# The order of the transposes, value projections and weight pieces in a slot-attention and FFN kernel, changed in one step

## Chip, cores and metric

The kernel runs on one core of a Trainium2 chip. The metric is the device time of one execution in microseconds; the time before is 1460.58 us, the median of three runs (1460.13 to 1461.77).

## What is computed

For four sequences of 512 tokens and 512 channels the program computes a pre-norm attention block over 64 slots (16 heads, key size 64, value size 128) and a pre-norm FFN with weights rounded to fp8, each with its residual. Cut to what matters:

```
q, k, v, s = x_ln @ Wq, x_ln @ Wk, x_ln @ Wv, clip(x_ln @ Ws, -32, 32)     # by heads
z = cumlogsumexp(s);  g = exp(z[t-1] - z[t]);  p = exp(s - z)
hk[t] = hk[t-1] * g[t] + k[t] p[t]^T;     ok[t] = (q[t] * 64**-0.5) @ hk[t]
hv[t] = hv[t-1] * g[t] + p[t] v[t]^T;     o[t]  = softmax(ok[t]) @ hv[t]
o = o * rsqrt(mean(o**2) + 1e-5) * g_norm * silu(x_ln @ Wg)
x = x + o @ Wo
x = x + ((silu(x_ln2 @ f8(gate) * gs) * (x_ln2 @ f8(up) * us)) @ f8(down)) * ds
```

## The kernel before

**Units.** The attention runs in 32 units (g, b): g is a pair of heads (0 to 7), b a sequence. All g run over the sequences 0 and 1 in turn, (0,0), (0,1), (1,0), (1,1) and so on, then all g over 2 and 3. A unit is one call of `attention` (the first is `first_unit`). v is projected for two pairs of heads at once, so that units of even g are **long** (they have four blocks of v, `X.values(0)` to `(3)`), and those of odd g are **short**. The output of a unit is finished in the next one: `before.scale_output`, `scale_other`, `turn_output`, `high_output`, `split_output`, `low_output`, `project_output` and `add_output` belong to the unit before. After the units comes the FFN.

**fp32 by parts.** A product of fp32 values is made from rounded parts: every weight matrix and every activation is held as a high part, a rest and a mixed part, and a projection (`Projection`) is eight 512-column matmuls (`main`, ps_s and so on) and four more (`mixed`, ps_s_m), in two PSUM tiles of the pool `proj`, which has three buffers. ACT reads the first (L525, for v L587), DVE subtracts the second (L547, for v L588).

**The head of a unit.** s is projected, clipped and exponentiated (eT), then k and q are projected. Beside them on DVE and ACT: the sums of squares of the last read-out (L796, L797), their power on POOL (L800), the scaling of the last output (`scale_output` L805 on DVE, `scale_other` L811 on ACT), and the scan z (L680) with its logarithm and reciprocal (L681, L682 on ACT). Then eT, kT and the two halves of the scaled output are transposed on PE (`turn_e` ps_e, `turn_k` ps_kn, `turn_output` ps_oT, four matmuls each), into three PSUM banks that are taken in turn (`bank`), and copied out: e (L692) and kn (L697) by ACT, the output by DVE (L834). `query_key` makes the four diagonal blocks a (ps_a; DVE L618), `key_states` the running sums sk (ps_sk; DVE L639 and L641, POOL L705).

**The tail.** Two gates (ps_g), the slot scores (ps_ok, okT L731), `value_states` (ps_sv), `softmax` (ps_okn, then DVE L738 and L740), the projected output of the unit before in four blocks (ps_o), `softmax_exp` (ACT), `slot_weights` (ps_w, wT L762), `weight_slot` (ps_b, DVE L618 again), `softmax_sum`, `read_out` (ps_ov).

**The list of pieces.** Work that isn't bound to a place stands in a list, `work`, and is issued in small pieces. `other(n)` issues the next n (or `pace[0]`), `piece()` issues until one that isn't a mere beginning, `need(name)` issues until none of that name is left. In the first half (b of 0 and 1) the pieces split the weights of the next units: `nm_` is the first high part on ACT (L256), `nm` one rest on DVE (L263 or L265, and L268), with the next high part and, where a buffer comes free, a fetch and the write of the parts by SP. They are put on the list by `load`: s, k, q and g in units with b = 1, v there too where g is even, o in units with b = 0. In the second half the parts are read back by DMA, and the pieces are the rounding of the FFN's weights ("round": `first`, `second`, `third`, two DVE instructions each, L463 to L477). Every engine takes its instructions in the order in which the program issues them, so that the place of `other` in the code is the place of the piece in its engine's queue.

**Layer norms.** The next sequence's normalised tokens (xn) are measured (m), normalised and transposed in four `steps`, taken by `next_step` or `early_step`; `step(n)` needs normalise(n), transposes (ps_xn L356) and puts the split of the parts (`xs_b`) and normalise(n+2) on the list. These steps run in (0,0), (7,0), (7,1), (0,2), (7,2), (7,3) and in the FFN. `turned()` says that an xs piece is next on the list. `pace[0]` is 2 in (0,1), (7,0), (0,2) and (7,2), else 1.

**Start.** The first sequence is fetched in four blocks by SP, with two halves of the first v matrix (`fetch`) behind block 0; block 0 is normalised, transposed and used for `values(0)` before block 1.

Of the kernel before, what the change touches and what calls it, by code (L numbers as in the profile page):

```python
# [49 lines left out]
def kernel(  # L50
# [268 lines left out]
    def layernorm(b, which, n_bank=None, first=None):  # L319
# [33 lines left out]
        def transposes(n):  # L353
            pt = bank(f"ps_xn{which}_{b}_{n}", n_bank).rearrange("p (c t) -> p c t", c=KC)
            for c in range(KC):
                nc.tensor.transpose(pt[:, c, :], xn[n][:, c * P : (c + 1) * P], ident)  # L356
            hi = dst[0][:, :, n * P : (n + 1) * P]
            if start:
                nc.scalar.copy(whole[0][:, :, n * P : (n + 1) * P], pt)
            elif which == 1:  # L360
                nc.scalar.mul(hi, pt, UNDER)
            else:
                nc.scalar.copy(hi, pt)
            pts[n] = pt
# [517 lines left out]
    def first_unit():  # L882
# [43 lines left out]
        next_step()  # L926
        next_step()
        X.softmax()
# [3 lines left out]
        X.slot_weights()  # L932
        other(1)
        X.gate_silu(0)
        X.gate_silu(1)
        exp_and_log()
        X.weight_slot()
        X.softmax_sum()
        need("xs_0")
        piece()  # L940
        piece()
# [3 lines left out]
    def attention(g, b, before, load, gated):  # L945
# [22 lines left out]
        def running_sum():  # L968
            before.scale_other()
            X.running_sum()  # L970
            if first:
                other(1)
            else:
                small()
# [5 lines left out]
        need("q")  # L980
        X.queries(other if even or turned() else None)
        load("q")
        X.turn_e()
        if even:
            X.turn_k()
            next_step()
            if turned():
                other(1)
            need("v")
            X.values(0)  # L990
            X.values(1)
            before.turn_output(0)
            before.high_output(0)
            before.turn_output(1)
            before.high_output(1)
            X.key_states()
            X.inverse()
            X.query_key()
            other()
            X.values(2)  # L1000
            before.split_output(0)
            next_step()
            other()
            X.values(3)
            other()
            next_step()
            before.split_output(1)
        else:
            before.turn_output(0)
            X.turn_k()  # L1010
            before.turn_output(1)
            before.high_output(0)
            before.high_output(1)
            X.query_key()
            X.key_states()
            before.split_output(0)
            before.split_output(1)
            X.inverse()
            if work and work[0][1] is scale_low:
                other(1)  # L1020
            if work and work[0][0] == "o":
                other()
# [21 lines left out]
        X.softmax()  # L1044
        if not turned():
            small()
        need("o")
        before.project_output(0)
# [13 lines left out]
        X.softmax_sum()  # L1062
        if even or b > 1 or steps:
            other()
        next_step()
        if turned():
            other(1)
        X.read_out()
        return X

# [80 lines left out]
    with tc.manual_schedule(engines=EVERY):  # L1151
        blocks = x[0].rearrange("(n p) d -> p n d", p=P)
        x1[0] = two.tile([P, NT, D], F32, tag="v", name="x1_0")
        for n in range(NT):
            nc.sync.dma_start(x1[0][:, n, :], blocks[:, n, :])
            if n == 0:
                fetch()
                fetch()
# [11 lines left out]
        for i, (g, b) in enumerate(units[1:], 1):  # L1170
# [44 lines left out]
            elif g % 2:  # L1215
                if not turned():
                    piece()
# [4 lines left out]
            else:  # L1222
                other(1)
                other(1)
            before = attention(g, b, before, load, gated)
# [90 lines left out]
```

## Time and profile before

The profiled execution took 1460.69 us; its span, from the first to the last instruction, is 1459.0 us, at a mean granted TensorE clock of 0.998.

| unit | start of ps_s, us | length to the next start, us |
|---|---|---|
| (0,1) long | 58.11 | 42.81 |
| (1,0) short | 100.92 | 30.95 |
| (1,1) short | 131.87 | 30.39 |
| (2,0) long | 162.26 | 41.13 |
| (2,1) long | 203.39 | 41.15 |
| (3,0) short | 244.54 | 30.97 |
| (3,1) short | 275.51 | 30.38 |
| (7,0) short, two steps | 531.74 | 32.76 |
| (7,1) short, two steps | 564.50 | 32.08 |
| (0,2) long, four steps | 596.58 | 43.54 |
| (0,3) long | 640.12 | 41.21 |
| (2,2) long | 742.09 | 41.57 |
| (2,3) long | 783.66 | 42.07 |
| (3,2) short | 825.73 | 30.38 |
| (7,2) short, two steps | 1114.75 | 32.17 |
| (7,3) short, two steps | 1146.92 | 31.37 to the first ps_fg at 1178.29 |

How to read the views: a line of the timeline has the start in us from the span's start, the time to the end of the last of the merged instructions, engine, source line, operation, what is written and read, shape, count, and in brackets how long the engine had been idle and what ended that. PE is the matmul engine, PEld its weight loads, DVE, ACT, POOL and SP the vector, scalar, GpSimd and sync engines. In the list of waits a line names who waited for whom, with the sum, the number and the longest of the waits in us.

### The profile page before, as it was taken

What the parts mean: (1) busy time and instruction counts of PE and PEld (TensorE: products, weight loads), DVE (VectorE), ACT (ScalarE), POOL (GpSimd) and SP (SyncE); (2) the same over time, 40 slices, a digit from 0 to 9 for tenths busy, and PEclk for the clock granted to TensorE, in tenths of its full rate; (3) what the DMA queues carried; (4) which work ended last, traced back from release to release, by engine and by line L of the source; (5) the groups of instructions that cost most, each with busy time, mean ns of one, the idle gap of its engine ahead of it and who ended that gap; (6) DMA issues with size and microseconds to landing.
All of it is one profiled execution on the core that took longest, in us unless ns stands there. A gap on an engine that the chain in (4) does not pass through costs nothing.

```text
span 1459.0 us, 22764 instructions
## 1 busy us (share of the span) xinstructions
PE 1431.5 (98%) x8875; PEld 1178.1 (81%) x8875; DVE 1105.6 (76%) x1966; ACT 711.0 (49%) x1214; POOL 242.4 (17%) x271
## 2 busy tenths in 40 slices
PE   8999999999999999999999999999999999999998
PEld 4688888888888888888888888888888888888886
DVE  6788768976897689878988898898889874445333
ACT  4556555555565556455544454456445643222221
POOL 2012211211121122211211121111112120000000
PEclk9999999999999999999999999999999999999999
DMA  8275456565656464456546654665465562101000
GB/s 332 78 226 176 143 159 172 174 191 157 173 173 191 128 231 123 138 159 188 159 116 188 202 166 102 195 202 168 129 180 174 148 178 28 59 0 58 1 29 29
DMA packets 80715, 212.51 MB, mean 146 GB/s; under 512 B 6152, under 2 KB 34848, under 8 KB 75424
## 3 DMA queue, kind: packets, MB, share of 16 engines
q1 hardware_dynamic: 62080, 177.49, 32.8%
q0 software_dynamic: 18528, 33.58, 15.7%
q8 instruction: 70, 1.15, 0.3%
q14 instruction: 37, 0.30, 0.1%
HBM read 107.23 MB, written 108.00 MB: 148 GB/s over the span
## 4 chain that ended last, share of the span: by engine, by line
PE 85%; DVE 10%; ACT 2%; issue 1%; DMA 1%; POOL 0%; SPq 0%; DVEq 0%; ACTq 0%
PE ps_o L861 8%; PE ps_g L520 8%; PE ps_v L579 7%; PE ps_fg L1077 6%; PE ps_fu L1077 6%; PE ps_o_m L861 4%; PE ps_ov L785 4%; PE ps_g_m L543 4%; PE ps_v_m L579 4%; PE ps_s L520 3%; PE ps_k L520 3%; PE ps_q L520 3%; PE ps_fd L1126 3%; PE ps_fe L1126 2%; PE ps_b L614 2%; PE ps_a L614 2%
## 5 line engine op out<-in xcount | busy, mean ns | idle before, releaser
L877 POOL DMA_DIRECT2D stream<-y x128 | 113.2, 893 | 471.5 <-DVE y L876 464.3
L861 PE MATMUL ps_o<-w_o,oT 128*128 128x512 f32 x512 | 144.8, 404 | 0.0
L520 PE MATMUL ps_g<-xs,w_g 128*128 128x512 f32 x496 | 125.2, 394 | 0.0
L579 PE MATMUL ps_v<-w_v,xs 128*128 128x512 f32 x480 | 122.4, 397 | 0.3 <-ACT v L587 0.3
L1098 DVE SCALAR_TENSOR_TENSOR h<-ps_fu,scol,act 128x512 f32<-128x512 f32 x48 | 36.0, 751 | 105.4 <-PE ps_fu L1077 104.1
L871 ACT ACTIVATE y<-ps_o 128x512 f32<-128x512 f32 x128 | 76.7, 599 | 73.9 <-PE ps_o L861 73.9
L520 PEld LDWEIGHTS ps_g<-xs,w_g 128*128 128x128 f32 x496 | 91.7, 188 | 19.8
L861 PEld LDWEIGHTS ps_o<-w_o,oT 128*128 128x128 f32 x512 | 91.5, 188 | 17.1
L579 PEld LDWEIGHTS ps_v<-w_v,xs 128*128 128x128 f32 x480 | 87.7, 188 | 19.5 <-ACT v L587 0.8
L705 POOL COPY sk_both<-sk 64x192 f32<-64x192 f32 x64 | 43.7, 682 | 344.6 <-DVE sk L641 342.7
L1077 PE MATMUL ps_fg<-xs,wf 128*128 128x512 f32 x384 | 96.5, 393 | 0.0
L1077 PE MATMUL ps_fu<-xs,wf 128*128 128x512 f32 x384 | 95.0, 389 | 0.0
L876 DVE TENSOR_TENSOR y<-y,ps_o_m 128x512 f32<-128x512 f32 x128 | 87.2, 682 | 10.1 <-ACT y L871 9.3
L587 ACT ACTIVATE v<-ps_v 128x512 f32<-128x512 f32 x60 | 35.9, 599 | 99.5 <-PE ps_v L579 99.5
L1077 PEld LDWEIGHTS ps_fu<-xs,wf 128*128 128x128 f32 x384 | 72.1, 188 | 15.2
L795 ACT ACTIVATE og<-ps_ov 128x512 f32<-128x512 f32 x64 | 38.1, 597 | 93.4 <-PE ps_ov L785 93.4
L1077 PEld LDWEIGHTS ps_fg<-xs,wf 128*128 128x128 f32 x384 | 71.1, 188 | 14.4
L588 DVE TENSOR_TENSOR v<-v,ps_v_m 128x512 f32<-128x512 f32 x60 | 41.1, 684 | 53.6 <-PE ps_v_m L579 53.6
L861 PE MATMUL ps_o_m<-w_o,oT 128*128 128x512 f32 x256 | 79.3, 391 | 0.2 <-ACT y L871 0.2
L1104 ACT CAST both<-h 128x512 fp32r<-128x512 f32 x48 | 29.8, 620 | 96.5 <-DVE h L1098 96.5
L800 POOL TENSOR_TENSOR rs<-rs,mhalf 128x8 f32<-128x8 f32 x32 | 59.2, 1850 | 86.5 <-DVE rs L797 48.4
L1095 ACT ACTIVATE act<-ps_fg,scol 128x512 f32<-128x512 f32 x48 | 33.0, 688 | 81.2 <-PE ps_fg L1077 81.2
(171 smaller groups left out, 3309.5 us busy)
## 6 DMA issues: line engine op xcount, KB each, us to landing
stream<-y POOLq DMA_DIRECT2D x128, 256.0 KB, 6.1
split_v<-w_v SPq DMA_DIRECT2D x4, 3072.0 KB, 14.7
split_g<-w_g SPq DMA_DIRECT2D x8, 1536.0 KB, 6.9
split_o<-w_o SPq DMA_DIRECT2D x8, 1536.0 KB, 6.2
w_v<-split_v SPq DMA_DIRECT2D x4, 3072.0 KB, 15.6
w_g<-split_g SPq DMA_DIRECT2D x8, 1536.0 KB, 6.5
w_o<-split_o SPq DMA_DIRECT2D x8, 1536.0 KB, 9.7
rounded<-qw SPq DMA_DIRECT2D x36, 256.0 KB, 3.9
```

The lines of the kernel that those rows point to most:

```text
L520: nc.tensor.matmul(self.p, products(self.nm, c, self.col0, i), xs[self.b][i][:, c, :], start=(i == 0 and c == 0), stop=(i == 1 and c == KC ...
L543: nc.tensor.matmul(self.m, products(self.nm, c, self.col0, 2), xs[self.b][2][:, c, :], start=(c == 0), stop=(c == KC - 1),)
L579: nc.tensor.matmul(dst, xs[b][i][:, c, n * P : (n + 1) * P], wt["v"][:, i, c * 2 * HV : (c + 1) * 2 * HV], start=(i == which[0] and c == 0 ...
L614: nc.tensor.matmul(pa[h][:, n, :], lT[rows, cols], rT[rows, cols], start=True, stop=True)
L785: nc.tensor.matmul(po[h][:, n, :], self.bb[h][:, n, :], both_v[self.b][:, n, self.v0 + h * DV : self.v0 + (h + 1) * DV], start=False, stop ...
L800: nc.gpsimd.tensor_tensor(rs, rs, mhalf.rearrange("p (h n) -> p h n", h=HG), ALU.pow)
L861: nc.tensor.matmul(dst, self.oT[:, i, h, n * P : (n + 1) * P], wt["o"][:, i, h * D : (h + 1) * D], start=(i == which[0] and h == 0), stop= ...
L871: nc.scalar.mul(y, p, 1.0 + DELTA)
L876: nc.vector.tensor_tensor(y, y, m, ALU.subtract)
L877: nc.gpsimd.dma_start(stream[self.b][n * P : (n + 1) * P, :], y, accum_op=ALU.add)
L1077: nc.tensor.matmul(pp, w[:, c * P : (c + 1) * P], xs[b][k][:, c, :], start=(c == 0 and k == 0), stop=(c == KC - 1 and k == 1),)
L1126: nc.tensor.matmul(sums[n], parts[k][:, n * P : (n + 1) * P], fw[c][2], start=(c == 0 and k == 0), stop=(c == NFC - 1 and k == 1),)
```

## The change

Six things are moved, none is added or left out of the computation.

1. Both kinds of unit now begin the same way after q: `turn_e`, `turn_output(0)`, `turn_k`, `turn_output(1)`, the two highs of the output, then (after the step of a layer norm, in long units) `query_key` and `key_states`. In long units the four blocks of v follow, with the output's splits and inverse between them; before, two blocks of v stood between the transposes of e and k and those of the output, and key states and a followed these.
2. Pieces in long units: the one between q's parts goes (unless an xs piece is due), one to three are issued after `values(0)` (three in (0,1), two for b of 2 and 3, one else), and for b of 2 and 3 one instead of two before the unit. In (0,1) none is left in `running_sum`.
3. Pieces elsewhere: short units with b = 0 lose the piece at their start; long units with b = 1, except the first, issue `piece()` for `other()` after softmax and after `softmax_sum`.
4. Steps of the layer norms: in short units of the first half the last step comes after `read_out`; in those of the second half it is dropped there, and an `early_step` is added after `key_states`.
5. `first_unit`: the fourth step goes from behind `value_states` to behind `slot_weights`, the xs piece that it makes is issued after `weight_slot`, and one `piece()` before the read-out goes.
6. Start: one half of v's matrix is fetched after block 0 and one after block 1, and the first copy of xn is made in two halves.

```diff
             if start:
-                nc.scalar.copy(whole[0][:, :, n * P : (n + 1) * P], pt)
+                for half in (0, 1) if n == 0 else (None,):
+                    cs = slice(None) if half is None else slice(half * KC // 2, (half + 1) * KC // 2)
+                    nc.scalar.copy(whole[0][:, cs, n * P : (n + 1) * P], pt[:, cs])
...
         X.value_states()
         next_step()
-        next_step()
         X.softmax()
         X.softmax_exp()
         other(1)
         X.gate_main(1)
         X.slot_weights()
-        other(1)
+        next_step()
         X.gate_silu(0)
         X.gate_silu(1)
         exp_and_log()
         X.weight_slot()
+        need("xs_1")
         X.softmax_sum()
         need("xs_0")
-        piece()
         piece()
         X.read_out()
...
             X.running_sum()
-            if first:
-                other(1)
-            else:
+            if not first:
                 small()
...
-        X.queries(other if even or turned() else None)
+        X.queries(other if turned() else None)
         load("q")
         X.turn_e()
+        before.turn_output(0)
+        X.turn_k()
+        before.turn_output(1)
+        before.high_output(0)
+        before.high_output(1)
         if even:
-            X.turn_k()
             next_step()
             if turned():
                 other(1)
+        X.query_key()
+        X.key_states()
+        if even:
             need("v")
             X.values(0)
+            other(3 if first else 2 if b > 1 else 1)
+            before.split_output(0)
             X.values(1)
-            before.turn_output(0)
-            before.high_output(0)
-            before.turn_output(1)
-            before.high_output(1)
-            X.key_states()
             X.inverse()
-            X.query_key()
             other()
             X.values(2)
-            before.split_output(0)
+            before.split_output(1)
             next_step()
             other()
             X.values(3)
             other()
             next_step()
-            before.split_output(1)
         else:
-            before.turn_output(0)
-            X.turn_k()
-            before.turn_output(1)
-            before.high_output(0)
-            before.high_output(1)
-            X.query_key()
-            X.key_states()
+            if b > 1:
+                early_step()
             before.split_output(0)
...
         X.softmax()
-        if not turned():
+        if even and b == 1 and not first and not turned():
+            piece()
+        elif not turned():
             small()
+        elif not even and b > 1:
+            other(1)
...
         X.softmax_sum()
-        if even or b > 1 or steps:
+        if even and b == 1 and not first and not turned():
+            piece()
+        elif even or b > 1 or steps:
             other()
-        next_step()
-        if turned():
-            other(1)
+        if even:
+            next_step()
+            if turned():
+                other(1)
         X.read_out()
+        if not even and b < 2:
+            next_step()
+            if turned():
+                other(1)
         return X
...
-            if n == 0:
-                fetch()
+            if n < 2:
                 fetch()
...
             elif g % 2:
-                if not turned():
+                if b > 0 and not turned():
                     piece()
...
             else:
-                other(1)
-                other(1)
+                other(1 if b > 1 else 2)
             before = attention(g, b, before, load, gated)
```

## The prediction

> **What bounds the kernel now.** I read the page's span and busy shares, then the list of PE's waits, then the timeline of PE for the start of every unit (its first ps_s row), and last the timeline of all engines inside units that run longer than their like.
>
> ```profile
> span 1459.0 us, 22764 instructions
> PE 1431.5 (98%) x8875; PEld 1178.1 (81%) x8875; DVE 1105.6 (76%) x1966; ACT 711.0 (49%) x1214; POOL 242.4 (17%) x271
> ```
> PE sets the end. In the timeline a group of eight 512-column matmuls starts 1.81 us before the next (ps_k 247.38, ps_k_m 249.19), 227 ns each, everywhere. The change adds and removes no PE work, so only PE's waits and the seams between its groups can move. The Trainium skill (Trainium Kernel Development and Optimization, Performance Expectations) calls matmul busy time a bad measure and weight-load busy time a good one; by its rule the 81% of PEld would leave 19% of the span, an estimated 277 us, to a better order, while the 227 ns pitch says that nothing of this is open here.
>
> ```profile
> PE ps_xn L356 <- DVE xn L349: 3.6, 4, 1.3
> PE ps_kn L596 <- DVE kT L547: 2.3, 4, 0.7
> PE ps_xn L356 <- DVE b L618: 2.0, 2, 1.2
> PE ps_oT L596 <- ACT e L692: 1.1, 3, 0.4
> ```
> Columns: total us, times, longest. The lengths of the units (start to start) show the rest: an undisturbed long unit takes 41.13 (162.26 to 203.39), a short one 30.38 (275.51 to 305.89). Over that are (0,1) by 1.7; (1,0), (3,0), (5,0) by 0.57 each; (2,2) 0.44, (2,3) 0.94, (4,2) 0.94, (4,3) 0.80, (6,2) 0.84, (6,3) 0.46; and the units with transposes of xn. The short units' 0.57 and the excess of the second half come from these rows, of the timeline of (3,0) and of (2,3):
>
> ```profile
> 244.54 2.09 PE L520 MATMUL ps_s<-xs,w_s 128*128 128x512 f32 x8
> 247.56 1.96 POOL L800 TENSOR_TENSOR rs<-rs,mhalf 128x8 f32<-128x8 f32 x1 [2.54 <-DVE rs L797]
> 250.50 1.23 DVE L680 TENSOR_TENSOR_SCAN z<-eT 128x512 f32<-128x512 f32 x1
> 252.54 0.63 ACT L682 ACTIVATE rzT<-rzT 128x512 f32<-128x512 f32 x1
> 253.08 0.61 ACT L256 ACTIVATE w_v<-raw_v 128x512 fp32r<-128x512 f32 x1
> 253.60 0.58 ACT L525 ACTIVATE qT<-ps_q 128x512 f32<-128x512 f32 x1
> 254.07 0.58 ACT L692 COPY e<-ps_e 128x512 f32<-128x512 f32 x1
> 254.71 0.66 PE L596 MATMUL ps_oT<-ident,og 128*128 128x128 f32 x4 [0.36 <-ACT e L692]
> ...
> 793.19 0.66 PE L596 MATMUL ps_kn<-ident,kT 128*128 128x128 f32 x4 [0.65 <-DVE kT L547]
> ```
> Four transposes in turn (e, oT0, kn, oT1) use three banks, so oT1 takes e's bank and starts 0.64 after the ACT copy of e does. That copy stands on ACT behind L682, any weight high (L256) and qT, and these hang on the DVE scan z. Undisturbed, oT1 starts 9.59 after the unit (e at +8.28, three groups of 0.44): **the copy of e must start by +8.95**. Here it starts at +9.53.
>
> **The change, part by part.** Times with + are from the unit's start; the price of a weight pair on DVE (L263, L268) is 1.33 (247.30, 248.02, next 248.63), of an ACT high 0.53.
>
> Long units, second half (b of 2 or 3). One DVE piece leaves the head (other(1) for two) and one leaves queries; both go behind values(0). Then the head is that of the short units (1,2) to (5,3), which have the same order and one piece there, and whose lengths are 30.31 to 30.39, without stall. All 0.44+0.94+0.94+0.80+0.84+0.46 = **-4.4** goes. What is late next is the DVE queue in the v blocks. From the start of the first v block (0): its L588 can run at 3.16 (793.60 to 796.69, and 0.07 for the seam), then two pieces (0.67, 1.06 or 1.33 each), split 1.33, L588 0.61, inverse 1.35, a piece, L588, split, a piece, the last L588. A third proj buffer must be free at 13.77. With the pieces third-first-second the last L588 starts at 13.36 and frees it at 13.96, else before: 0.2 in (0,3), (2,3), (4,3), **+0.6**. Below, nothing; above, with all four pieces at 1.33, 1.15 a unit. Behind a waiting L588 on DVE stand the split of the output and inverse; who waits for them is ACT's low_output and okT, both behind the gates, 5 us later. The moved pieces take their SP issues along (0.34 for a split write, 0.37 for a fetch); no wait of PE names these. On POOL sk_both comes 8 us earlier in long units, ahead of stream adds that are issued much later: 0.
>
> Seams. Old long order over bare matmuls: e 0.44, kn 0.35, v +0.10, oT pair 0.96, sk 0.50, a 1.09, v +0.14 = 3.58. The short order: 0.44+0.44+0.44+0.55+1.09+0.50+0.16 = 3.62. 15 long units at 0.04: **+0.6**.
>
> Long units of the first half with b=1: (2,1), (4,1), (6,1). Their head is unchanged, two o pairs, and in the old order nobody waited for e's copy, since kn was followed by v. Now oT1 does. The timeline of (2,1):
>
> ```profile
> 203.39 2.09 PE L520 MATMUL ps_s<-xs,w_s 128*128 128x512 f32 x8
> 211.64 0.63 ACT L682 ACTIVATE rzT<-rzT 128x512 f32<-128x512 f32 x1
> 212.18 0.61 ACT L256 ACTIVATE w_s<-raw_s 128x512 fp32r<-128x512 f32 x1
> 212.70 0.58 ACT L525 ACTIVATE qT<-ps_q 128x512 f32<-128x512 f32 x1
> 213.18 0.58 ACT L692 COPY e<-ps_e 128x512 f32<-128x512 f32 x1
> ```
> The copy starts at +9.79, so oT1 at 10.43 for 9.59: 0.84. Their softmax piece now puts two highs on ACT ahead of exp, 0.1 more. Three units: **+2.8**. (2,0), (4,0), (6,0) have the copy at 9.08, after a high that queries issued and no longer does; less 0.5 it is on time: 0.
>
> (3,0), (5,0): the piece at their start goes (b > 0), and the new tail piece of (2,1) leaves rs where it was (L797 at +2.68). Then POOL's pow binds L805: 5.18 becomes 5.05, 0.13 each; up to 0.3 with the 4.89 of (7,0). **-0.3**.
>
> (1,0): without the start piece, the first v pieces fall to running_sum: v_ is an ACT high behind L682, and the DVE pair waits for it ahead of kT. z at +5.78, L682 7.82, high 8.36 to 8.97, pair 9.0 to 10.33, kT to 11.0; kn at 11.0 for 9.16, oT1 at 11.45 for 10.17: **+1.3**. (1,1) then inherits v at its start, o_ with o at running_sum, and o behind inverse: high 7.54 to 8.15, pair, kT to 10.2, kn +1.05; the late o pair holds okT as in (7,1), where sv to okn is 1.62 for 0.96: **+1.7**.
>
> In all of these the low end is 0, if the piece comes sooner than I count, and the high end half as much again, if qT is late with it.
>
> (0,1): DVE work 1.33 shorter ahead of rs, no high before qT, but three pairs behind v block 0; the e stall falls from 0.23 and the v_m waits (0.50 and more) go; new waits by the same count as above 0.05+0.6+0.5, and 0.25 at oT1. 1.7 becomes 1.5: **-0.2**, between -0.9 and +1. (0,2): measure, parts and n2 come between the transposes and a on DVE, some 2.5 us; a's reader pok comes 14 us later: 0.
>
> (0,0): x block 1 is fetched ahead of half of raw_v. Its landing (DVE's stats wait for it to 9.68) stops binding, but measure(2) stands before normalise(1) on DVE, and block 2 lands as before, some 7.7 after its issue at 2.7 (the blocks take 7.5 in the median, 7.9 at most), at 10.4; 1.0 of measure and 0.6 of normalise later the transposes start at 12.04 for 12.29, **-0.25**; the halved copy of xn feeds a v product that isn't on this path: 0. One xn step moves from before okn to behind w. okn needs okT at 47.75, now 48.73: 1.0, of which 0.44 is the xn now in the hole from w to b (52.64 to 54.02): **-1.0**.
>
> The granted clock was 0.50 from 15.27 to 18.69, after a stretch with PE busy 1.82 of 3.41: 1.7 lost, which I leave where it is; gone or doubled it is -1.7 or +1.7. The Trainium skill (TensorE: Matmul & The Clock Gate, Part 1) says that the window runs free of the program; by it the sum could shift by that estimate either way without cause in the code.
>
> (7,0), (7,2): step 1 held the read-out behind b (1.53 and 0.95 in ps_b, 1.23 of it as idle before ps_xn). In (7,0) it goes behind read_out; 1.1 comes back, but DVE is full through (7,1) to its ps_a at +11.25, and gives only what rs gains, 0.5: **-0.5**. (7,2) **-1.1**. Step 3 of (7,3) now stands behind key_states and calls normalise(3) there: on DVE behind both a and three sk.
>
> ```profile
> 1159.26 1.29 DVE L618 TENSOR_TENSOR a<-ps_a,tri 128x512 f32<-128x512 f32 x2 [0.33 <-PE ps_a L614]
> 1159.66 2.14 PE L520 MATMUL ps_g<-xs,w_g 128*128 128x512 f32 x8
> 1160.71 0.48 DVE L641 TENSOR_TENSOR sk<-ps_sk,sk 128x64 f32<-128x64 f32 x2
> ```
> PE is free at 1159.66; DVE ends sk at 1161.1, normalise takes 0.54: PE stands 2.0. With 0.15 at oT1: **+2.15**.
>
> Sum: -4.4-0.3-0.2-0.25-1.0-0.5-1.1 = -7.75; +0.6+0.6+2.8+1.3+1.7+2.15 = +9.15; net +1.4. The profiled execution took 1460.69 (span 1459.0 and 1.69 around it), 0.11 over the median 1460.58: 1462.1, or **1462.0** beside the median. FFN: no edit reaches it, and its weights come as before.
>
> **The rivals.** *Faster (1456.2).* The late pieces I found in heads don't bind: the weight highs are ready before I place them, so (1,0), (1,1), (2,1), (4,1), (6,1) keep their lengths: 1462.0 less 2.8, 1.3 and 1.7 is 1456.2. For: the head of short units bears one pair. Against: the rows above have the high between L682 and qT, and (3,0) shows oT1 waiting at +9.53. *Slower (1467.3).* The v blocks: DVE's in-order queue holds L588 and so the proj buffers; from a last L588 later than 13.1 each unit pays. With 0.35 in each of 15 long units, 1462.0+5.3. For: all DVE idle time of the old v blocks (2.29, 2.04) is spent by then. Against: my count leaves 0.1 to 1.5 to spare in most. *No effect of the head:* the second-half stalls stay, because kT is late by the running_sum piece and not the head's: 1466.4. Against: short units with that piece have none.
>
> **How the numbers follow.** A measurement here tells 0.2% (2.9 us) from nothing. Within it (1457.7 to 1463.5): 0.48, its own range 1459.5 to 1463.5. Faster 0.22. Slower: v blocks 0.20, head 0.10. Two in ten left out, with the clock's 1.7: 1456.0 to 1466.0.
>
> **What would show it.** After: no wait of kn for kT in (2,2) to (6,3); oT1 waiting 0.8 for e in (2,1), (4,1), (6,1); kn waiting for kT over 1 us in (1,0) and (1,1); xn waiting 2 us for L349 in (7,3); (0,0) 1.2 shorter. Wrong if the v blocks show ps_v or ps_g waiting for DVE v L588 in many units, or if these waits are absent.

## The result, and the profile after

The changed kernel takes 1466.14 us (median of six runs, 1464.88 to 1466.58), the kernel before on the same chip 1460.16 (six runs, 1458.67 to 1461.77). The ratio is 1.0041, with a 95% interval of 1.0031 to 1.0051: **slower by 0.4%**. The profiled execution took 1466.44 us, its span is 1464.7. The page of the changed kernel, span and busy times:

```profile
span 1464.7 us, 22809 instructions
PE 1434.7 (98%) x8875; PEld 1178.8 (80%) x8875; DVE 1108.7 (76%) x1966; ACT 710.6 (49%) x1215; POOL 230.0 (16%) x271
```

The engines do the same work as before. (PE's 3.2 us more are no more matmuls: the count is equal. Each of the two profiles has one stretch of 3.41 us at half clock inside the program, so that this isn't the difference.) The list of PE's waits, changed kernel; lines of the code from 361 on stand two further down than before, so that L596 is now L598 and L547 is L549:

```profile
PE ps_xn L356 <- DVE xn L349: 3.5, 3, 2.1
PE ps_oT L598 <- ACT e L694: 2.4, 4, 0.7
PE ps_kn L598 <- DVE kT L549: 2.1, 2, 1.2
...
PE ps_g_m L545 <- ACT sg L527: 1.4, 1, 1.4
...
PE ps_g_m L545 <- ACT v L589: 0.9, 1, 0.9
```

Three things are read from it. kn waits for kT 2 times now, not 4, and the sum is hardly less; but these are other places: the four of before stood in the second half and are gone, the two of now stand in (1,0) and (1,1). oT waits for e 2.4 us in place of 1.1, in (0,1), (2,1), (4,1) and (6,1). And two waits stand here that the list of before doesn't have: the gates' ps_g_m for ACT, once 1.4 and once 0.9 us. The unit lengths (start of ps_s to the next), with the forecast's term beside what came:

| place | before | after | forecast | measured |
|---|---|---|---|---|
| from the span's start to the first ps_s | 20.39 | 17.87 | -0.25 | -2.51 |
| (0,0) | 37.73 | 36.81 | -1.0 | -0.91 |
| (0,1) | 42.81 | 45.99 | -0.2 | **+3.18** |
| (1,0), (1,1) | 30.95, 30.39 | 31.72, 32.11 | +1.3, +1.7 | +0.77, +1.73 |
| (2,1), (4,1), (6,1) | 41.15 each | 42.20 each | +0.98 each | +1.05 each |
| (2,0), (4,0), (6,0) | 41.13 each | 41.21 each | +0.04 each | +0.08 each |
| (3,0), (5,0) | 30.96 each | 30.37 each | -0.15 each | -0.60 each |
| (7,0), (7,1) | 32.76, 32.08 | 31.73, 33.10 | -0.5 in sum | -0.01 in sum |
| (0,2), (0,3) | 43.54, 41.21 | 43.73, 41.41 | +0.3 in sum | +0.39 in sum |
| (2,2), (2,3), (4,2), (4,3), (6,2), (6,3) | 251.20 in sum | 248.44 | -3.75 | -2.76 |
| (7,2) | 32.17 | 30.73 | -1.1 | -1.45 |
| (7,3) | 31.37 | 36.24 | +2.15 | **+4.87** |
| FFN | 280.70 | 280.71 | 0 | +0.01 |

The two bold rows lie 6.1 us over their terms. That is more than the whole miss (the span grew by 5.7, the forecast was 1.4), because the start came out 2.3 lower than forecast. First (7,3). The timeline of the changed kernel there:

```profile
1160.85 1.29 DVE L620 TENSOR_TENSOR a<-ps_a,tri 128x512 f32<-128x512 f32 x2 [0.33 <-PE ps_a L616]
...
1162.31 0.48 DVE L643 TENSOR_TENSOR sk<-ps_sk,sk 128x64 f32<-128x64 f32 x2
1162.71 0.54 DVE L349 TENSOR_SCALAR xn<-x,mv,rstd 128x512 f32<-128x512 f32 x1
...
1163.39 0.63 PE L356 MATMUL ps_xn<-ident,xn 128*128 128x128 f32 x4 [2.07 <-DVE xn L349]
1163.78 3.24 PE L522 MATMUL ps_g<-xs,w_g 128*128 128x512 f32 x8
```

The wait is the one forecast (2.0; it is 2.07): normalise(3) stands on DVE behind a and three sk. What was not forecast is the line under it: the eight matmuls of ps_g take 3.24 in place of 2.11. The busy times in two stretches of the changed kernel (PE, PEld, DVE, ACT, POOL busy with counts, then the granted clock, the share of the DMA engines, GB/s):

```profile
1160.98:1164.40 3.42, 1.35 (x19) 1.15 (x16) 3.32 (x8) 0.55 (x2) 1.22 (x2) 1.00 0.05 20
1164.40:1167.82 3.42, 3.42 (x10) 2.64 (x9) 2.93 (x5) 1.01 (x3) 0.00 (x0) 0.50 0.00 0
```

After a stretch of 3.42 us with PE busy for 1.35, the clock is half for the next 3.42: here the idle time is paid nearly twice.

Then (0,1). The timeline of the kernel before, the fetches of the next two raw matrices and the one high that waits for them:

```profile
70.64 0.37 SPq L213 DMA_DIRECT2D raw_k<-in_L_attn_Wk_dram  x1
...
80.03 0.37 SPq L213 DMA_DIRECT2D raw_q<-in_L_attn_Wq_dram  x1
...
82.99 0.63 ACT L256 ACTIVATE w_q<-raw_q 128x512 fp32r<-128x512 f32 x1 [1.04 <-DMA raw_q<-in_L_attn_Wq_dram]
```

The timeline of the changed kernel where the gates begin:

```profile
77.83 0.37 SPq L213 DMA_DIRECT2D raw_k<-in_L_attn_Wk_dram  x1
...
79.13 2.11 PE L522 MATMUL ps_g<-xs,w_g 128*128 128x512 f32 x8 [0.51 <-DVE v L590]
...
80.99 0.63 ACT L256 ACTIVATE w_k<-raw_k 128x512 fp32r<-128x512 f32 x1 [5.45 <-DMA raw_k<-in_L_attn_Wk_dram]
81.08 0.37 SPq L213 DMA_DIRECT2D raw_q<-in_L_attn_Wq_dram  x1
81.53 0.58 ACT L589 ACTIVATE v<-ps_v 128x512 f32<-128x512 f32 x1
82.16 1.20 PE L545 MATMUL ps_g_m<-xs,w_g 128*128 128x512 f32 x4 [0.92 <-ACT v L589]
...
85.46 0.63 ACT L256 ACTIVATE w_q<-raw_q 128x512 fp32r<-128x512 f32 x1 [3.36 <-DMA raw_q<-in_L_attn_Wq_dram]
86.00 0.58 ACT L527 ACTIVATE sg<-ps_g 128x512 f32<-128x512 f32 x1
86.63 1.19 PE L545 MATMUL ps_g_m<-xs,w_g 128*128 128x512 f32 x4 [1.44 <-ACT sg L527]
```

Read upwards from each row of ps_g_m: PE waits for a PSUM evacuation on ACT; that waits in ACT's queue behind the high part of a weight (L256); that waits for its DMA; and the DMA was issued late. The DMA is issued by a piece (`rest` calls `fetch`), so that whoever postpones a piece postpones a transfer. Before the change raw_k was fetched 12.5 us after the start of (0,1) (70.64), now 23.1 after it. PE's waits of over 0.2 us in (0,1) are four: 0.92 and 1.44 at the end of this chain, 0.51 at the first gate for DVE's part of v, and 0.44 in the head, where oT waits for e. Before there was one, of 0.34.

### The profile page after: what moved, and what is told of

It is laid out like the page before. It is cut to its first block, busy times and chain, and to the rows that moved or that the text cites. A ratio compares the mean times of both kernels' runs of the same rounds, so it can differ in the third digit from the quotient of the medians.

```text
span 1464.7 us, 22809 instructions
## 1 busy us (share of the span) xinstructions
PE 1434.7 (98%) x8875; PEld 1178.8 (80%) x8875; DVE 1108.7 (76%) x1966; ACT 710.6 (49%) x1215; POOL 230.0 (16%) x271
## 4 chain that ended last, share of the span: by engine, by line
PE 86%; DVE 9%; ACT 3%; issue 2%; DMA 0%; POOL 0%; DVEq 0%; POOLq 0%; SPq 0%; ACTq 0%
PE ps_o L863 8%; PE ps_g L522 8%; PE ps_v L581 7%; PE ps_fg L1084 6%; PE ps_fu L1084 6%; PE ps_ov L787 4%; PE ps_g_m L545 4%; PE ps_o_m L863 4%; PE ps_v_m L581 4%; PE ps_s L522 3%; PE ps_q L522 3%; PE ps_k L522 3%; PE ps_fd L1133 3%; PE ps_fe L1133 2%; PE ps_a L616 2%; PE ps_b L616 2%
## 5 line engine op out<-in xcount | busy, mean ns | idle before, releaser
L522 PEld LDWEIGHTS ps_g<-xs,w_g 128*128 128x128 f32 x496 | 91.7, 189 | 22.2 <-ACT sg L527 1.3
L707 POOL COPY sk_both<-sk 64x192 f32<-64x192 f32 x64 | 33.2, 519 | 280.6 <-DVE sk L643 278.8
L527 ACT ACTIVATE sg<-ps_g 128x512 f32<-128x512 f32 x62 | 37.0, 597 | 81.2 <-PE ps_g L522 53.2
```

What stands on the lines that cost most here:

```text
L522: nc.tensor.matmul(self.p, products(self.nm, c, self.col0, i), xs[self.b][i][:, c, :], start=(i == 0 and c == 0), stop=(i == 1 and c == KC ...
```

## The experiments

Each is the changed kernel with the edit shown, except where it says "before". Ratios are against the kernel before, run on the same chip.

### e1: the pieces of (0,1) back

```diff
             X.running_sum()
-            if not first:
+            if first:
+                other(1)
+            else:
                 small()
...
-        X.queries(other if turned() else None)
+        X.queries(other if first or turned() else None)
...
-            other(3 if first else 2 if b > 1 else 1)
+            if not first:
+                other(2 if b > 1 else 1)
```

> The changed kernel with the pieces of unit (0,1) alone back where they were: one in running_sum, two in queries, none behind values(0); the order of transposes, a, states and v stays the new one. Theory (late fetch: SP's fetch of raw_k hangs on the postponed pieces, so the highs L256 of k and q wait 5.4 and 3.4 us for their DMA on ACT, ahead of the evacuations L589 and L527): raw_k is fetched about 7 us sooner, no L256 waits over 1 us for a DMA, (0,1) goes from 45.99 to 42.9 us, the whole from 1466.1 to 1463.0. Rival (the new order itself: DVE's queue is too full in the four v blocks of (0,1), whose pace is two pieces a place): (0,1) stays at 45 or more, the whole within 1 us of 1466.1.

Measured: 1465.59 us, ratio 1.0035 (1.0022 to 1.0048); (0,1) 45.59. raw_k is still fetched 22.7 us after the unit's start (77.22), ACT still waits 3.57 and 3.36 us for raw_k and raw_q, and the head pays besides (kn waits 0.50 for kT, oT 0.76 for e, a 0.40 for qT). **The theory fell in this form**, and the number of the rival came (45 or more): the places of the pieces in (0,1) alone don't bring the fetch forward. In the list, g's last piece still stands ahead of o's.

### e2: the steps of (7,2) and (7,3) as in the first half

```diff
-            if b > 1:
-                early_step()
             before.split_output(0)
...
-        if not even and b < 2:
+        if not even:
             next_step()
```

> The changed kernel with the steps of the layer norm in (7,2) and (7,3) as in the first half: step 1 of (7,2) after read_out, no early_step behind key_states. Theory (late normalise, and PE idle for 2 us opens a window of half clock): (7,3) goes from 36.24 to about 31.5 us, (7,2) from 30.73 to 31.6 with an xn more in it, no half clock after 1160 us; together -3.9, the whole 1462.2. Rival (the half clock is free of the program and stays, there or elsewhere): -2.2 alone, 1463.9.

Measured: 1462.39 us, ratio 1.0019 (1.0010 to 1.0029); (7,3) 31.66, (7,2) 31.18, and the granted clock is 1.00 from 1161 to 1171 us. In sum 4.1 us less, as the theory says.

### e3: one piece, not two, in the heads of (2,1), (4,1), (6,1)

```diff
-                other(1 if b > 1 else 2)
+                other(1 if b > 0 else 2)
             before = attention(g, b, before, load, gated)
...
-            other(3 if first else 2 if b > 1 else 1)
+            other(3 if first else 2 if b > 0 else 1)
```

> The changed kernel with one piece in place of two before the long units (2,1), (4,1), (6,1), the other behind values(0), as the change does in the second half. Theory (the head bears one pair on DVE, not two): kn no longer waits for kT, the three units go from 42.20 to 41.2 us each, the whole -3.0, 1463.1. Rival (the price only moves: the pair makes the first v evacuation L590 and the gates late): -1.5 or less, the units at 41.7 or more.

Measured: 1463.67 us, ratio 1.0025 (1.0016 to 1.0035); the units take 41.35, 41.35 and 41.33, 0.86 less each. The timeline of (2,1), first of the changed kernel:

```profile
213.97 0.63 ACT L684 ACTIVATE rzT<-rzT 128x512 f32<-128x512 f32 x1
214.51 0.61 ACT L256 ACTIVATE w_s<-raw_s 128x512 fp32r<-128x512 f32 x1
215.03 0.58 ACT L527 ACTIVATE qT<-ps_q 128x512 f32<-128x512 f32 x1
215.51 0.57 ACT L694 COPY e<-ps_e 128x512 f32<-128x512 f32 x1
216.14 0.66 PE L598 MATMUL ps_oT<-ident,og 128*128 128x128 f32 x4 [0.64 <-ACT e L694]
```

then of this run:

```profile
212.65 0.63 ACT L684 ACTIVATE rzT<-rzT 128x512 f32<-128x512 f32 x1
213.19 0.60 ACT L527 ACTIVATE qT<-ps_q 128x512 f32<-128x512 f32 x1
214.54 0.59 ACT L694 COPY e<-ps_e 128x512 f32<-128x512 f32 x1 [0.75 <-PE ps_e L598]
215.21 0.62 PE L598 MATMUL ps_oT<-ident,og 128*128 128x128 f32 x4
```

The high L256 is gone from between L684 and qT, the copy of e now waits for PE and not the other way round, and the bracket behind ps_oT is gone. The wait in the head is the one forecast.

### e4: the piece at the start of (1,0) back

```diff
-                if b > 0 and not turned():
+                if (b > 0 or g == 1) and not turned():
                     piece()
```

> The changed kernel with the piece at the start of the short unit (1,0) back ((3,0) and (5,0) stay without). Theory (the v pair must not fall to running_sum, where its high stands behind L682): (1,0) from 31.72 to 30.9 and (1,1) from 32.11 to 30.4 us, the whole -2.5, 1463.6. Rival (v's high is late because its raw half is fetched late, at 101.5, in unit (0,1)): (1,0) and (1,1) keep 1 us or more of their excess, the whole 1465 or more.

Measured: 1463.87 us, ratio 1.0027 (1.0017 to 1.0036); (1,0) 30.93, (1,1) 30.39, both as before the change, 2.5 us in sum. The timeline of (1,0) in the changed kernel shows the chain that this removes, high, rest, kT, kn:

```profile
107.90 0.63 ACT L684 ACTIVATE rzT<-rzT 128x512 f32<-128x512 f32 x1
108.43 1.14 ACT L256 ACTIVATE w_v<-raw_v 128x512 fp32r<-128x512 f32 x2
109.08 0.69 DVE L263 TENSOR_TENSOR w_v<-raw_v,w_v 128x512 fp32r<-128x512 f32 x1 [1.88 <-ACT w_v L256]
...
110.42 0.68 DVE L549 TENSOR_TENSOR kT<-kT,ps_k_m 128x512 f32<-128x512 f32 x1
...
111.15 0.65 PE L598 MATMUL ps_kn<-ident,kT 128*128 128x128 f32 x4 [1.16 <-DVE kT L549]
```

DVE stands idle for 1.88 us ahead of the rest, because its high part waits on ACT behind the scan's logarithm and reciprocal. The rival, which left 1 us or more of the excess in place, fell.

### e5: the dropped piece of (0,0) back

```diff
         need("xs_0")
+        piece()
         piece()
         X.read_out()
```

> The changed kernel with the one piece() before the read-out of (0,0) back, which the change drops; (0,1) keeps its new places. Theory, mended after the run with the pieces of (0,1) put back (its raw_k was still fetched 22.7 us after the unit's start, against 12.5 before): the whole list runs one item late, because of that dropped piece; the three places behind values(0) then hold o_, o, o instead of g, o_, o, so raw_k is fetched by +20 us, the ACT waits for raw_k and raw_q (5.4 and 3.4) fall under 1, and (0,1) goes from 45.99 to 43.5 us; (0,0) grows by 0.5 at most; the whole from 1466.1 to 1464.0. Rival (the places in (0,1) decide, the fetch stays late): (0,1) 45.5 or more, the whole 1466 or more.

Measured: 1464.53 us, ratio 1.0034 (1.0023 to 1.0045); (0,1) 44.80, between the two expectations; (0,0) unchanged. The timeline of (0,1) of this run:

```profile
74.29 0.37 SPq L213 DMA_DIRECT2D raw_k<-in_L_attn_Wk_dram  x1
77.31 0.63 ACT L256 ACTIVATE w_k<-raw_k 128x512 fp32r<-128x512 f32 x1 [0.60 <-DMA raw_k<-in_L_attn_Wk_dram]
...
81.85 0.63 ACT L256 ACTIVATE w_q<-raw_q 128x512 fp32r<-128x512 f32 x1 [2.34 <-DMA raw_q<-in_L_attn_Wq_dram]
...
83.48 2.11 PE L522 MATMUL ps_g<-xs,w_g 128*128 128x512 f32 x8 [0.90 <-DVE v L590]
```

The wait for raw_k is 0.60 in place of 5.45, and at the gates PE waits once, for DVE, whose queue is full from 71.65 on. The two waits behind transfers (0.92 and 1.44) are gone, but the piece's pair of DVE instructions now stands ahead of the head of (0,1): q waits 0.51 for eT, and oT 0.93 for e in place of 0.44. The piece back is thus worth 1.2 us net of the 3.2.

This run also has what became the test of the clock. Its (7,3) has the same waits as the changed kernel and takes 34.61, not 36.24. The stretches of this run:

```profile
1157.16:1160.57 3.41, 2.25 (x35) 1.82 (x32) 3.04 (x7) 1.80 (x3) 0.00 (x0) 1.00 0.66 261
1160.57:1163.99 3.42, 2.51 (x13) 2.19 (x14) 3.32 (x7) 0.59 (x1) 1.22 (x2) 1.00 0.00 0
1163.99:1167.40 3.41, 3.41 (x16) 2.82 (x15) 2.06 (x4) 2.25 (x5) 0.00 (x0) 1.00 0.00 0
```

The same idle time falls on the border of two stretches, neither is below 2.25, and the clock stays at 1.00. The half clock is 1.63 us of (7,3) here. Four more profiles have the same 2.07 us wait in (7,3) and a half clock behind it: in e1, e3, e4 and e6 the unit takes 36.06 to 36.25.

### e6: both (e1 and e5)

The edits are those of e1 and e5 together.

> Both put back: the piece() of (0,0) and the places of the pieces in (0,1). Theory (list one item late): raw_k is fetched 12 to 14 us after the unit's start as before the change, no ACT wait for it, but two o pairs burden the head, where oT1 waits for e: (0,1) 43.2 to 43.9 us, the whole 1464.3. Rival (the new order of transposes before v is the cause): (0,1) 45 or more.

Measured: 1467.16 us, ratio 1.0054 (1.0039 to 1.0069); (0,1) 47.31, the longest so far, an estimated 1.7 of it (half of 3.41) by a half clock (70.0 to 73.4). The number of the rival came. raw_k is fetched 13.4 us after the unit's start and the v blocks show no wait, but the head does. Its timeline:

```profile
66.49 0.62 ACT L256 ACTIVATE w_o<-raw_o 128x512 fp32r<-128x512 f32 x1
67.01 0.57 ACT L694 COPY e<-ps_e 128x512 f32<-128x512 f32 x1
67.63 0.65 PE L598 MATMUL ps_oT<-ident,og 128*128 128x128 f32 x4 [1.94 <-ACT e L694]
68.80 0.68 DVE L549 TENSOR_TENSOR qT<-qT,ps_q_m 128x512 f32<-128x512 f32 x1
69.53 1.72 PE L616 MATMUL ps_a<-qT,kT 64*128 64x128 f32 x16 [1.25 <-DVE qT L549]
```

Here the pieces stand where they stood before the change, ahead of qT on DVE, and qT comes 14.0 us after the unit's start, little later than before (13.15: 71.26 for 58.11). Before, nobody asked for it then: two blocks of v stood ahead of a. So early pieces hurt the head in the new order, and late pieces delay the fetch. The fetch needs both the piece of (0,0) and the early places: 23.1 us after the unit's start in the changed kernel, 22.7 with the places alone (e1), 19.8 with the piece alone (e5), 13.4 with both. This gave the theory its third form, for e9.

### e7: before, with the new order for b of 2 and 3 alone

```diff
-        X.queries(other if even or turned() else None)
+        X.queries(other if even and b < 2 or turned() else None)
...
-        if even:
+        if even and b > 1:
+            before.turn_output(0)
+            X.turn_k()
...
+            X.values(0)
+            other(2)
...
+        elif even:
             X.turn_k()
...
-                other(1)
-                other(1)
+                other(1 if b > 1 else 2)
```

> The kernel before with the new order and places of pieces in the long units of b 2 and 3 alone; all else as before. Theory (the gain of the second half stands by itself): (2,2), (2,3), (4,2), (4,3), (6,2), (6,3) are 2.8 us shorter in sum, (0,2) and (0,3) 0.4 longer in sum; the whole -2.4 against before: 1457.6. Rival (the gain came from the short units' steps or from the start and doesn't stand alone): within 0.7 us of before.

Measured: 1456.89 us, ratio 0.9984 (0.9974 to 0.9994). The six units are 2.78 us shorter in sum, as in the changed kernel, (0,2) and (0,3) 0.26 longer. The second half's gain stands by itself.

### e8: four parts put back (e2 to e5)

The edits are those of e2, e3, e4 and e5 together.

> The changed kernel with four parts put back: the piece() of (0,0), the start piece of (1,0), one piece for two in the heads of (2,1), (4,1), (6,1), and the steps of (7,2), (7,3) as in the first half. Theory (the losses are local and add): 2.5+2.5+2.6+4.1 less than 1466.1, 1454.4. Rival (what one part saves is lost in the next, as the pieces are one list): above 1457.

Measured: 1455.90 us, ratio 0.9975 (0.9966 to 0.9985). Each unit has the length that it had in the run of its own edit, to 0.1 us: (0,1) 44.81, (1,0) 30.93, (1,1) 30.39, (2,1) 41.36, (7,2) 31.13, (7,3) 31.68. The losses are local and add; 1.5 above the sum expected, of which (0,1) is 1.3.

### e9: e8 with the old order in (0,1) alone

```diff
         X.turn_e()
+        if first:
+            X.turn_k()
+            need("v")
+            X.values(0)
+            X.values(1)
         before.turn_output(0)
-        X.turn_k()
+        if not first:
+            X.turn_k()
         before.turn_output(1)
...
+        if first:
+            X.key_states()
+            X.inverse()
+            X.query_key()
...
```

(with the pieces of e1 and the other two blocks of v behind)

> The run with four parts put back (e8), and unit (0,1) alone in the old order with its old places of pieces: e and kn, two blocks of v, then the output, sk, a, two blocks of v. Theory, third form for (0,1): the three weight pairs of this unit take 4 us of DVE wherever they are put, and in the old order two blocks of v (5.44 us of PE) stood between the transposes and a, which reads qT; this cover, not a place of a piece, is what the change takes away. (0,1) from 44.81 to 42.8 to 43.1 us, the whole from 1455.9 to 1454.0. Rival (the moved xn step of (0,0) makes the head of (0,1) late): (0,1) 43.8 or more.

Measured: **1453.80 us, ratio 0.9965 (0.9952 to 0.9978), the lowest of all runs** (the intervals of e8 and e10 overlap with it). (0,1) takes 43.70, between the two expectations: 1.11 less than in e8, and 0.89 more than before the change. raw_k is fetched 13.4 us after the unit's start. In (0,0) and (0,1) this run has the pieces of e6 and differs from it by the order alone: e6's waits of 1.94 at oT and 1.25 at a are not there, and after q PE waits for no more than before the change. What is left over stands at the head:

```profile
60.96 0.68 DVE L549 TENSOR_TENSOR eT<-eT,ps_s_m 128x512 f32<-128x512 f32 x1
61.70 2.11 PE L522 MATMUL ps_q<-xs,w_q 128*128 128x512 f32 x8 [0.51 <-DVE eT L549]
```

eT is 5.8 us after the unit's start, against 4.95 before (63.06 for 58.11): DVE comes out of (0,0) 0.87 later, since the parts of the moved xn step now stand behind b, ahead of the sums of squares. Of the 0.89, 0.27 stands at the second part of s and the rest at q. So the moved step gains 0.92 in (0,0) and gives back 0.89 in (0,1). In the changed kernel itself q doesn't wait: with one piece fewer ahead of it, eT comes 4.5 us after the unit's start. Both theories of this run had a part.

### e10: before, with the parts that gained

```diff
-                if not turned():
+                if (b > 0 or g == 1) and not turned():
                     piece()
...
-        next_step()
-        if turned():
-            other(1)
+        if even or b < 2:
+            next_step()
...
         X.read_out()
+        if not even and b > 1:
+            next_step()
...
```

(with e7's edit, and the change's `piece()` for `other()` in the tails of long units with b = 1 and its `other(1)` after softmax in short units of the second half)

> The kernel before with the parts that gained: the new order in long units of b 2 and 3, the start pieces of (3,0) and (5,0) dropped with piece() for other() in the tails of long units of b 1, and the last step of (7,2) behind read_out; start, (0,0) and all long units of the first half as before. Theory (gains are local and add): against before -2.4 by the second half, -1.1 by (3,0) and (5,0), -0.7 by (7,2) and (7,3): 1455.4, if (2,1), (4,1), (6,1) keep 41.15. Rival (piece() in the tails makes the long units 0.2 longer, or (3,0) keeps its 0.57): 1456.5 or more.

Measured: 1454.68 us, ratio 0.9970 (0.9958 to 0.9982). (3,0) and (5,0) lose 0.65 and 0.58, (7,2) 1.00; (2,1), (4,1), (6,1) take 0.12 to 0.16 more, (7,3) 0.28 more. Start, (0,0) and the order of the first half are as before, so that none of these is needed for the gain.

### e11: before, with the edits of (0,0) alone

```diff
         X.value_states()
         next_step()
-        next_step()
...
         X.slot_weights()
-        other(1)
+        next_step()
...
         X.weight_slot()
+        need("xs_1")
         X.softmax_sum()
         need("xs_0")
-        piece()
         piece()
```

> The kernel before with the edits of (0,0) alone: the fourth xn step behind slot_weights, its parts behind weight_slot, one piece() less before the read-out. Theory: (0,0) from 37.73 to 36.8 us, and (0,1) in the old order bears the list one item late: the fetch of raw_k comes 10 us later and the highs of k and q wait for it on ACT, so (0,1) is 1 to 2.5 us longer; the whole within 1.6 above and 0.3 below before. Rival (the list one item late costs nothing in the old order): (0,1) keeps 42.8, the whole 0.9 below before.

Measured: 1460.75 us, ratio 1.0013 (1.0003 to 1.0022). (0,0) 36.81, and (0,1) 46.96 in the old order, an estimated 1.7 of it by a half clock. The timeline of this run (line numbers of before):

```profile
78.17 0.37 SPq L213 DMA_DIRECT2D raw_k<-in_L_attn_Wk_dram  x1
81.32 0.63 ACT L256 ACTIVATE w_k<-raw_k 128x512 fp32r<-128x512 f32 x1 [4.00 <-DMA raw_k<-in_L_attn_Wk_dram]
...
86.19 0.63 ACT L256 ACTIVATE w_q<-raw_q 128x512 fp32r<-128x512 f32 x1 [3.75 <-DMA raw_q<-in_L_attn_Wq_dram]
...
87.36 1.42 PE L543 MATMUL ps_g_m<-xs,w_g 128*128 128x512 f32 x4 [1.83 <-ACT sg L525]
```

The fetch of raw_k is 22.2 us after the unit's start, nearly as in the changed kernel, though the order and the places of (0,1) are the old ones: the edits of (0,0) alone make it late, and of these it is the dropped piece, since e9 has the same moved step with the piece kept, and 13.4. A gain of 0.91 in one unit costs some 2.5 in the next, and more where the clock follows.

### e12: the normalise of (7,3) ahead of a

```diff
+        if not even and b > 1:
+            while work and work[0][0][:2] in ("xs", "xn"):
+                other(1)
         X.query_key()
         X.key_states()
```

> The changed kernel with the steps of (7,3) where the change puts them, but the normalise that the third of them needs issued on DVE ahead of a and sk. Theory (what costs in (7,3) is that normalise stands behind a and sk on DVE, and the half clock follows from the idle time): xn waits under 0.5, no half clock, (7,3) from 36.24 to 33.0 us, the whole 1462.9. Rival (a, 0.5 later on DVE, then holds sk and the gates as long): (7,3) 34.5 or more.

Measured: 1461.87 us, ratio 1.0020 (1.0010 to 1.0029); (7,3) 32.49. The timeline of this run:

```profile
1160.80 0.54 DVE L349 TENSOR_SCALAR xn<-x,mv,rstd 128x512 f32<-128x512 f32 x1
...
1161.61 0.66 PE L356 MATMUL ps_xn<-ident,xn 128*128 128x128 f32 x4
```

With the normalise half a microsecond ahead of a on DVE, xn has no wait, no clock is lost there, and a's later start holds nobody. The step's place on PE was harmless; what it waited for on DVE was not. (In this run a stretch of (0,1) had PE busy for 1.51, followed by a half clock, and the unit took 2.0 more: some 0.5 by a longer wait for sg, 1.90 for 1.44, and the rest by the clock.)

## Why the prediction was wrong

1462.0 was forecast, with "within 0.2%" the likeliest; 1466.14 came, 0.1 above the range of 1456.0 to 1466.0. The waits named as signs came, in (1,0) and (1,1) with 1.16 and 0.97 (over 1 was forecast), in (2,1), (4,1), (6,1) with 0.64 to 0.66 and in (7,3) with 2.07, and those of kn for kT left the second half. Two terms failed, (0,1) and (7,3), and several small ones were mis-sized.

**The term of (0,1), "-0.2, between -0.9 and +1", failed.** It came out at +3.18. The step that failed is the price of a moved piece. The forecast counted DVE's two instructions for each and laid down for the second half that "no wait of PE names" the SP issues that move with them. For (0,1) it took the same without looking, and so put the late transfer at nothing. There the piece is the one that fetches the next raw matrix, which is needed in the same unit. In its place the runs showed two waits of PE behind late transfers, 0.92 and 1.44, which go when the piece of (0,0) is put back (e5). The trace of before had the row: ACT waited 1.04 for raw_q, so that the cover was already thin, with raw_q fetched at 80.03 for a high at 82.99. The price of a piece is what it issues, on every queue, and the wait of whoever reads that.

Put back one after another, the parts of (0,1) bring this: 1.19 by the piece of (0,0) (e5: 45.99 to 44.80); 1.11 by the old order with its places of pieces (e8 to e9: 44.81 to 43.70); and 0.89 is left over against before, which the late eT of e9 puts down to the moved xn step of (0,0). These are net figures of the runs and not three waits of the changed kernel: the last is a wait for eT only where the piece is back.

**The second of these is cover lost.** Head work ahead of qT (3 pairs, 4 us of DVE) was hidden by two blocks of v between the transposes and a. With that work in its old places, the new order waits 3.2 us at oT and a (e6) and the old order doesn't (e9). The changed kernel avoids it by postponing the pieces, and pays at the gates. The forecast asked for this cover at e's copy and found 0.84 in (2,1), rightly, but not at qT, which no unit with fewer pieces shows.

**The term of (7,3), +2.15, was right in its wait (2.07 for 2.0) and mis-sized by the rest:** 0.74 at the head's transposes for the 0.15 put down, 0.41 for the four transposes of xn that move here from (7,2), which the term leaves out, and 1.63 by the half clock. With e12's normalise ahead of a, the wait and the half clock go. The forecast left the clock "where it is" with 1.7 either way, and argued from a rule that it shifts "without cause in the code". The runs show a cause: it follows a stretch in which PE had little to do, and with this edit there was one in (7,3) in five of six profiles.

**The second half: mechanism right, size off by 1.0.** The stall of kn is gone in all six units (e7 shows it alone). 4.4 were to go and 0.6 to come. What came is 1.66 over six times 41.13: the seams cost 0.08 or more each, not 0.04 (41.21 in (2,0), where PE has no new wait; 41.26 in (2,2)), and delays of 0.06 to 0.18 at the gates and in the last block of v came in four units, not in two.

**(1,0) and (1,1):** +1.3 and +1.7 were forecast, +0.77 and +1.73 came, and e4 takes both away with the one piece named. **(2,1), (4,1), (6,1):** 0.98 forecast, 1.05 measured, taken away by e3 but for 0.2. **(0,0):** -1.0 against -0.91, right by itself; what it costs in (0,1) was not asked. **(3,0), (5,0):** the direction held, the size was four times as large (-0.60): the whole excess went with the start piece, and with it the 0.36 for which oT waited for e; the power on POOL, which was to keep most of it, didn't. **(7,0), (7,1):** what (7,0) gains (1.03), (7,1) gives back in full (1.02), with kn waiting 0.61 and oT 0.10 in its head; half was expected to stay.

**The start is not settled.** The change's -2.51 compares one profile of before, which had a half clock at 15.27, with one of after, so that part of it is luck. From the first matmul to the first ps_s, four profiles with the old start show 15.67 to 18.84 us, ten with the new one 15.66 to 16.79. Whether the edits of the start bring anything can't be told from these.

**The rivals.** Of the slower one, "the v blocks", the symptom came (L590 holds a gate in (0,1) for 0.51), but at one place, beside 2.36 by way of a DMA, not 0.35 in each of fifteen units. The faster one fell with e3 and e4: the late pieces in heads do bind.

## What to carry to other kernels

A postponed piece of work postpones all that it issues, and the DMA that it starts may be wanted sooner than its arithmetic: look up for every moved piece which transfer hangs on it, and who waits at the end of that chain. An order that looks looser (long matmul blocks between the transposes and their readers) can be the cover of late work elsewhere, so change the order only where the late work is gone; here the new order gained in the second half and lost where two or three weight pairs stood in the head. And count a stall of 2 us on PE as possibly 3.6, as in (7,3) here: the clock may charge for it once more.

## What the hardware showed that was not expected

The half clock has a visible cause. In the record of each profile the changes of the clock lie on one grid with a pitch of 3.41 us, whose place differs from execution to execution. Between the first 10 and the last 10 us, nine stretches on this grid had PE busy for 1.09 to 1.82 us of 3.41 (1.09 and 1.38 in e6, 1.35 in the changed kernel, 1.44 in e4, 1.51 in e12, 1.58 in e11, 1.71 in e1, 1.76 in e3, 1.82 before), and each was followed by one stretch, and only one, at 0.50. Stretches with 1.95, 1.97 and more were not. So the same stall costs some 1.6 us more or nothing, by where the grid happens to cut it: e5 against the changed kernel. At both ends of the program the bound doesn't hold: 1.69, 1.81 and 1.83 in the first recorded stretch of e9, of before and of e10, and 1.51 and 1.76 near the last matmul of the changed kernel and of e5, were not followed by a half clock, while 1.42 at the end of before and 1.10 at the end of e6 were. What the clock looks at is thus not just the busy time that the profile shows; no run here says what else.

The Trainium skill (TensorE: Matmul & The Clock Gate, Part 1) says that the clock goes down after at least one idle window of about 3.4 us, and that the window runs free of the program. The free grid agrees with the runs. But no idle window is needed: one in which PE was half busy was enough.

In e6, e11 and e12 the half clock came in (0,1). In e11 and e12 one wait of 1.83 and 1.90 us was enough; in e6 two waits, of 1.94 and 1.25, lie close together and act as one.
